# Three products of batch 1 split once more by Strassen's scheme, in a hand-scheduled cross-attention and LoRA feed-forward kernel

## The chip, the core and the metric

The kernel runs on one core of a Trainium2 chip. A core has five engines that work side by side: TensorE (PE in the profile) multiplies, with its weight loads in rows of their own (PEld); VectorE (DVE) and ScalarE (ACT) do arithmetic on tiles; GpSimd (POOL) does small things; SyncE (SP) issues every DMA of this kernel, in one queue, in order. Tiles lie in SBUF with 128 partitions; TensorE writes its sums to PSUM, of which the kernel has 8 banks of 128 x 512 fp32. The metric is the device time of one execution in microseconds (us). Each time given is the median of several runs, or, where it is said, the time of the one execution that the profiler recorded.

## The reference

Inputs are x (2 x 1024 x 2048), a context ctx (2 x 2048 x 2048), two scales and zero points, a weight W (2048 x 2048) with bias, a router (8 x 2048) and LoRA matrices A (8 experts x 16 x 2048) and B (8 x 2048 x 16). Cut to what matters:

```python
q = lambda v, s, z: (clip(round(v / s + z), 0, 255) - z) * s
x = x + q(layernorm(x), s1, z1) @ q(ctx, s2, z2)       # per batch: 1024x2048 @ 2048x2048
y = layernorm(x)
w = top-2 of softmax(y @ W_router.T), normalised, spread over the 8 experts
lora = einsum('ter,eor,te->to', einsum('td,erd->ter', y, A), B, w) * 2
x = x + y @ W.T + bias + lora                          # 1024x2048 @ 2048x2048
```

The second product is the expensive one. The kernel keeps y and W as two fp16 halves each (a high part and the rest), so that every product of y and W is three fp16 products: low*high, high*low and high*high.

## The kernel before

The two batches follow each other. In each, the first product (`gemm1` in batch 0, `gemm1w` in batch 1) is added to x, the rows are normalised, `y_prep` makes the left operands of the second product, and `g2` multiplies them with W.

The second product uses one level of Strassen's scheme (in Winograd's form). A block is a pair p of 128-row tiles (4 pairs), 2048 inner rows cut in halves of 8 x 128, and 1024 output columns cut in halves of 512. The outputs are done in two passes f = 0 and f = 1 of 1024 columns each (`cp`); batch 0 takes cp 0 and then 1, batch 1 cp 1 and then 0. In place of 8 products of blocks there are 7, with the left operands a11, a12, a22, s1, s2, s3, s4 (tiles `y_<name>`, made by `y_prep`: normalise, add, split in two fp16 halves (`nat`), turn by a DMA transpose) and right operands of sums of W's blocks, made by `w_step` for every inner step k. The seven stand in four groups (`GROUPS`); a group runs over 8 steps k, within it over the 4 pairs p, and each (k, p, product) is three matmuls of 512 columns (line 1407). At the end of a group `EVAC` has VectorE add PSUM banks to the output tiles (line 1435, `xr`), and `LORA` adds the LoRA product (line 1423). In pass 0 the last group is X += a22 @ (the fourth sum of W); in pass 1 a22 stands in the third group beside s3, and a12 alone in the fourth.

`w_step` loads rows of W in fp32, forms the sums on VectorE, scales and rounds the high half (`hi`, line 444, ACT or DVE) and makes the low half (`lo`, line 1211, DVE). Of pass 1 of batch 0 it writes fp16 halves to DRAM (`store_w`, tiles `made`), and pass 0 of batch 1, which needs the same sums, loads those (`w <- made`).

x itself is written to DRAM (`spill`) when y is made and comes back as `xr` (`reload`) for the last additions; `put` writes the finished rows out.

What sets the order: nothing is written down by hand. Every operation is a task with an engine, a guessed duration, the buffers it reads and writes and a due time `prio`. `Plan.order` (line 184) plays the program through with these guesses, keeps a heap of events, and at each moment gives each free engine the most urgent task that is ready and finds its buffers. The tasks are then issued in the order of their planned starts; on the chip every engine keeps its order and waits only for what it needs. The guesses are the constants at the head of the file: `RATE` the DMA rate, `LAND`, `STORE_LAND`, `TURN_LAND` the time from the last byte to the semaphore, `TURN_COST` and `TURN_ISSUE` the transposes. All big tiles share 49 buffers of 4 KB per partition (`SLOTS["u"]`); three narrow tiles (`byte`) are handed out in turn.

## Time and profile before

| | us |
|---|---|
| median of 3 runs (lowest, highest) | 912.36 (911.86, 913.17) |
| the profiled execution | 910.92 |
| its span, first to last instruction | 909.1 |
| PE busy in it | 896.0 (99%) |
| DVE busy | 708.0 (78%) |
| ACT busy | 388.7 (43%) |
| DMA queue 1, share of 16 engines' span | 86.8% |
| granted TensorE clock, mean | 1.00 |

A line of the groups reads: line of the kernel, engine, operation, tile written, tiles read, shapes, how many | busy time in us, mean ns of one | idle time before them and what ended it. Matmuls are pipelined: one of 512 columns lasts 379 ns in the records but the next one starts after 216. What a matmul costs is therefore read from a run of them in the timeline: the time of the run less one duration, over the number less one. In the table of windows a row gives a stretch, its length, and for each engine its busy time and number of instructions, then the granted clock, the DMA engines' mean share and GB/s.

### The profile page before, as it was taken

How to read it: one execution, taken by the hardware profiler on the slowest of the kernel's cores; microseconds unless marked ns; L12 is line 12 of the kernel's file. 1: busy time of each engine (PE TensorE's matmuls, PEld its weight loads, DVE VectorE, ACT ScalarE, POOL GpSimd, SP SyncE). 2: the span in 40 equal slices, each digit the busy share in tenths (PEclk: the TensorE clock that was granted, in tenths of full speed). 3: DMA queues.
4: the chain of work that ended last, by engine and by line, in shares of the span. 5: the costliest groups of instructions: out<-in, count | busy, mean ns of one | idle time of the engine just before them, and what ended most of it. 6: DMA issues, size and time to landing. Idle time of an engine off the chain costs nothing.

```text
span 909.1 us, 12499 instructions
## 1 busy us (share of the span) xinstructions
PE 896.0 (99%) x4542; PEld 432.4 (48%) x4542; DVE 708.0 (78%) x1305; ACT 388.7 (43%) x445; POOL 47.4 (5%) x199
## 2 busy tenths in 40 slices
PE   8899999999999999999999999999999999999998
PEld 6344446474444444444444444556444444444443
DVE  8989999999499966999889979999543363899131
ACT  4875976525144221323686776754100021324000
POOL 1014000000000000002540000000000000000000
PEclk9999999999999999999999999999999999999999
DMA  9999999998999999999999748999994169883021
GB/s 327 387 386 278 348 285 225 245 265 226 255 362 325 314 395 406 380 369 345 301 343 323 243 170 235 228 169 222 308 283 109 50 224 371 288 337 134 6 93 46
DMA packets 223917, 241.02 MB, mean 265 GB/s; under 512 B 146032, under 2 KB 158320, under 8 KB 223856
## 3 DMA queue, kind: packets, MB, share of 16 engines
q1 hardware_dynamic: 223856, 240.23, 86.8%
q8 instruction: 35, 0.57, 0.3%
q14 instruction: 26, 0.21, 0.1%
HBM read 163.65 MB, written 41.94 MB: 226 GB/s over the span
## 4 chain that ended last, share of the span: by engine, by line
PE 85%; DVE 9%; DMA 3%; issue 1%; SPq 1%; ACT 0%; DVEq 0%; ACTq 0%
PE X L1406 34%; PE Y L1406 27%; PE g L829 11%; PE gX L949 3%; PE ph L1067 3%; PE gY L949 2%; DVE x L858 2%; PE X L1423 2%; PE Y L1423 2%; PE ph L1071 1%; DMA x<-in_x_dram 1%; DVE byte L455 1%; DMA bs<-in_cx_dram 1%; DVE sm L478 1%; DVE bt L920 1%
## 5 line engine op out<-in xcount | busy, mean ns | idle before, releaser
L1406 PEld LDWEIGHTS <-y_s 128*128 128x128 f16 x1536 | 150.3, 98 | 181.0
L1406 PE MATMUL Y<-w,y_s 128*128 128x512 f16 x768 | 206.6, 379 | 0.0
L1406 PE MATMUL X<-w,y_s 128*128 128x512 f16 x768 | 206.3, 379 | 0.0
L1406 PE MATMUL X<-w,y_a 128*128 128x512 f16 x768 | 189.1, 379 | 0.2 <-DVE w L1211 0.2
L1406 PEld LDWEIGHTS <-y_a 128*128 128x128 f16 x1152 | 112.1, 98 | 132.6 <-issue 0.5
L829 PE MATMUL g<-b,at 128*128 128x512 f16 x512 | 112.5, 379 | 4.7 <-DVE b L469 3.6
L1406 PE MATMUL Y<-w,y_a 128*128 128x512 f16 x384 | 103.2, 379 | 0.0
L444 ACT ACTIVATE w<-wb,gW 128x1024 f16<-128x1024 f32 (+1 forms) x46 | 50.0, 1091 | 111.1 <-DVE wb L1282 32.9
L1435 DVE SCALAR_TENSOR_TENSOR xr<-X,uW,xr 128x512 f32<-128x512 f32 x64 | 46.8, 746 | 46.9 <-PE X L1423 25.7
L829 PEld LDWEIGHTS <-at 128*128 128x128 f16 x512 | 49.7, 98 | 64.3 <-issue 4.2
L1435 DVE SCALAR_TENSOR_TENSOR xr<-Y,uW,xr 128x512 f32<-128x512 f32 x42 | 31.1, 745 | 53.8 <-PE Y L1423 53.8
L1211 DVE SCALAR_TENSOR_TENSOR w<-wb,gW,w 128x1024 f16<-128x1024 f32 (+1 forms) x48 | 57.0, 1194 | 6.0 <-ACT w L444 5.9
L444 ACT ACTIVATE byte<-bs,sc,rec 128x1024 uint8<-128x1024 f32 x40 | 48.3, 1236 | 13.5 <-DMA bs<-in_cx_dram 8.6
L444 ACT ACTIVATE w<-wt,gW 128x1024 f16<-128x1024 f32 x15 | 17.0, 1145 | 78.5 <-DVE wt L1258 38.7
L478 DVE BATCH_NORM_STATS2 sm<-x 128x6 f32<-128x512 f32 x64 | 40.9, 683 | 5.5 <-ACT q L444 4.2
L877 ACT ACTIVATE byte<-x,sm 128x1024 uint8<-128x1024 f32 x32 | 36.4, 1139 | 10.4 <-DVE x L858 6.8
L444 ACT ACTIVATE nat_s<-yt_a 128x1024 f16<-128x1024 f32 x31 | 31.9, 1049 | 20.0 <-DVE yt_a L1026 14.7
L949 PEld LDWEIGHTS <-at 128*128 128x128 f16 x256 | 25.0, 98 | 29.8
L1026 DVE TENSOR_TENSOR yt_a<-yt_a,yt_a 128x1024 f32<-128x1024 f32 x32 | 38.7, 1221 | 0.0
L1018 DVE TENSOR_TENSOR nat_s<-yt_a,nat_s 128x1024 f16<-128x1024 f32 x32 | 38.2, 1224 | 0.0
L1067 PE MATMUL ph<-ar,y_a 128*128 128x272 f16 x192 | 35.7, 279 | 0.0
L1071 PE MATMUL ph<-ar,y_a 128*128 128x136 f16 x192 | 34.6, 223 | 0.0
(196 smaller groups left out, 1107.1 us busy)
## 6 DMA issues: line engine op xcount, KB each, us to landing
bs<-in_cx_dram SPq DMA_DIRECT2D x64, 512.0 KB, 10.5
wt<-in_wT_dram SPq DMA_DIRECT2D x64, 512.0 KB, 7.4
wn<-in_wT_dram SPq DMA_DIRECT2D x32, 512.0 KB, 9.1
x<-in_x_dram SPq DMA_DIRECT2D x30, 512.0 KB, 8.4
spill<-x SPq DMA_DIRECT2D x28, 512.0 KB, 4.4
xr<-spill SPq DMA_DIRECT2D x28, 512.0 KB, 8.5
wb<-in_wT_dram SPq DMA_DIRECT2D x24, 512.0 KB, 7.8
out_dram<-xr SPq DMA_DIRECT2D x24, 512.0 KB, 4.0
```

Source lines behind the costliest of these rows:

```text
L444: nc.scalar.activation(o, i, AF.Copy if c is None else AF.Identity, scale=1.0 if a is None else a, bias=0.0 if c is None else c,)
L478: nc.vector.bn_stats(st[:, 2 * h + c], b.ap()[:, c * C : (c + 1) * C])
L829: nc.tensor.matmul(ps.ap(), aT.ap()[:, k, :], S["b", c, k // 4].ap()[:, k % 4, :], start=k == 0, stop=k == KT - 1,)
L877: nc.scalar.activation(low(sq), xb.ap(), AF.Square, bias=a[:, 22 + j : 23 + j], accum_out=a[:, 24 + 2 * j + h : 25 + 2 * j + h],)
L949: nc.tensor.matmul(ps.ap(), a()[:, 4 * h + k, :], w.ap()[:, k, :], start=fresh and h + k == 0, stop=h == 1 and k == 3, skip_group_check=True,)
L1018: lambda: nc.vector.tensor_tensor(n.ap()[:, 1], t.ap(), n.ap()[:, 0], ALU.subtract),
L1026: add("DVE", 1.22, lambda: nc.vector.tensor_tensor(dst.ap(), a.ap(), c.ap(), op), r=[a, c], w=[dst])
L1067: nc.tensor.matmul(ph.ap()[:, : 2 * AR], y[half].ap()[:, 0, k, :], ar[:, kr, :], start=kk == 0, stop=False,)
L1071: nc.tensor.matmul(ph.ap()[:, AR : 2 * AR], y[half].ap()[:, 1, k, :], ar[:, kr, :AR], start=False, stop=kk == KT - 1,)
L1211: lambda: nc.vector.scalar_tensor_tensor(w.ap()[:, 1, lo:up], src(), g, w.ap()[:, 0, lo:up], ALU.mult, ALU.subtract),
L1406: nc.tensor.matmul(ps.ap(), y.ap()[:, a, k, :], w.ap()[:, q, j * C : (j + 1) * C], start=k == 0 and fresh and i == 0, stop=k == HK - 1 and ...
L1435: nc.vector.scalar_tensor_tensor(xs, ps.ap(), uW[:, cp : cp + 1], xs, ALU.mult, ALU.add)
```

## The change

1. Three of the fourteen block products of batch 1 (pass 0: a22; pass 1: a22 and a12) are no longer done by `g2` in its last group but by a new function `quarters`, which splits each once more: pairs of row pairs (2q, 2q+1), inner halves of 4 x 128, column halves of 256. Seven products of quarters take the place of eight; each is 12 matmuls of 256 columns (4 inner steps, three fp16 products) into a bank `X2`, `Y2` or into `X`. `LEVEL2` says which; `TABLE`, with a third entry in `GROUPS`, `LORA` and `EVAC`, leaves a22 and a12 out of pass 1's groups.
2. Their left operands are made by `y_quarters` from x, read back from `spill`: two extra turned tiles per pair of pairs and product (`q31`, `q24`). The four tiles a12 are written to DRAM in pass 0 (`y_out`) and read again in pass 1 (`y_in`).
3. Their right operands come from DRAM: a12's from W, a22's from two sums of W in fp32, which batch 0 stores (`store_t4`, tiles `t4`). Batch 0's pass 0 also reads its own third group's partial sum back (`wb <- t4`) instead of forming it again from rows of W. Pass 1's third group in batch 1 loads two 512-column pieces (`ws`) and makes one sum.
4. The scheduler: other constants; a store that is read later counts as done 2 us later; a transpose occupies the DMA from another moment; a `byte` tile goes back when its last user is issued, not in turn.

The diff, cut:

```diff
@@ -71,7 +71,16 @@
 PACE = .9
 TURNS = 4
 FAST = 4
-TMM = 0.12
+TMM = 0.08
+MM2 = 0.1095
+LEVEL2 = {(0, 0): (), (0, 1): (), (1, 0): ("a22",), (1, 1): ("a22", "a12")}
+TABLE = {(0, 0): 0, (0, 1): 1, (1, 0): 0, (1, 1): 2}
+YOUT = ((), ("a12",))
+T4 = (True, True)
+YO_T = 10.0
+YFAR = 60.0
+YQ = ((), ("a22", "a12"))
+SLOW_Q = 1.2
 SP_D = 10.0
 HC = 4.0
 PUT = 10.0
@@ -88,17 +97,20 @@
 SP_T = 5.0
 HOP = 0.7
 DMA_SLACK = 3.0
-RATE = 374e3
+RATE = 390e3
 SLOW_W = 1.18
 SLOW_C = 1.03
-LAND = 2.1
-STORE_LAND = 1.15
-TURN_LAND = 0.65
-TURN_COST = 1.0
-TURN_ISSUE = 1.5
+LAND = 1.5
+STORE_LAND = 1.35
+STORE_WAIT = 2.0
+TURN_LAND = 0.97
+TURN_COST = 1.35
+TURN_WHOLE = 1.95
+TURN_HEAD = {1: 0.9, 2: 1.6}
+TURN_ISSUE = 1.4
 RING = 5
 MERGE = 2.5
-WHOLE_ISSUE = 1.8
+WHOLE_ISSUE = 2.0
 TURN_RING = 2
 NEXT = {"DVE": 0.08, "ACT": 0.1}
 
@@ -290,7 +302,9 @@
                                 if room < 0 or len(group) > 1:
                                     end = max(end, at)
                                     break
-                        dma_free = max(end + 0.2, dma_free) + t.dma * len(group)
+                        begin = now + (TURN_HEAD[len(group)] if t.turn else t.dur + 0.2)
+                        dma_free = max(begin, dma_free) + (
+                            TURN_WHOLE if len(group) > 1 else t.dma)
                         done = dma_free + (
                             TURN_LAND if t.turn else STORE_LAND if t.store else LAND
                         )
@@ -321,7 +335,7 @@
                                     wake(b.last)
                         for x in t.succs:
                             x.left -= 1
-                            x.ready = max(x.ready, t.done)
+                            x.ready = max(x.ready, t.done + (STORE_WAIT if x.store and x.succs else 0.0))
                             if not x.left:
                                 for e in x.durs:
                                     bisect.insort(ready[e], (x.prio, x.seq, x))
@@ -357,9 +371,7 @@
 
     def byte(name):
         def make():
-            ring = rings["byte"]
-            ring.append(ring.pop(0))
-            return ring[-1]
+            return rings["byte"].pop(0)
 
         return Buf("byte", make, 1, name)
@@ -993,6 +1005,61 @@
...
+    def y_quarters(S, b, q, o):
+        yt = []
+        j = int(o[1]) - 1
+        for p in (2 * q, 2 * q + 1):
+            s = S["s2", p]
+            d = S["spill", 2 * p + j, 1]
+            t = buf("u", [P, HD], F32, f"yq_{o}_{b}_{p}")
+            load(t, t.ap, d.ap, HD * 4, [t], r=[d])
+            affine(t.ap, t.ap, HD, [(s, [j])], [t], scale=lambda s=s: s.ap()[:, 10 + j : 11 + j],
+                   bias=lambda s=s: s.ap()[:, 12 + j : 13 + j])
+            yt.append(t)
+        a, c = yt
+        lo = lambda t: t.ap()[:, :C]
+        up = lambda t: t.ap()[:, C:]
+
+        def comb(dst, x, y, op, r, w):
+            add("DVE", 0.69, lambda: nc.vector.tensor_tensor(dst(), x(), y(), op), r=r, w=[w])
+
+        comb(lambda: up(c), lambda: lo(c), lambda: up(c), ALU.add, [], c)
+        comb(lambda: lo(c), lambda: lo(a), lambda: lo(c), ALU.subtract, [a], c)
+        comb(lambda: lo(a), lambda: up(c), lambda: lo(a), ALU.subtract, [c], a)
+        comb(lambda: up(a), lambda: up(a), lambda: lo(a), ALU.subtract, [], a)
+        y_emit(S, b, 2 * q, o + "q31", c)
+        y_emit(S, b, 2 * q, o + "q24", a)
+
@@ -1043,7 +1095,7 @@
         emit("s4", t5)
         for i in (2 * p, 2 * p + 1):
             for h in range(2):
-                if h == b and p >= SPILL0:
+                if h == b and p >= SPILL0 and f"a{1 + i % 2}2" not in YQ[b]:
@@ -1170,11 +1222,20 @@
             hh.ap().rearrange("p t h c -> p (t h c)")))
 
     made = {}
+    whole_t4 = {}
     STORED = {
         0: ((1, 1, 1),),
         1: ((0, 0, 1), (1, 1, 2)),
-        2: ((0, 0, 3), (1, 0, 2)),
+        2: ((0, 0, 3), (1, 0, 2)) if "a22" not in LEVEL2[1, 0] else ((1, 0, 2),),
...
+    def store_t4(k, cp, s, cap):
+        if cp not in whole_t4:
+            whole_t4[cp] = Buf(
+                "dram", lambda: dram.tile([P, HK, C], F32, name=f"t4_{cp}"), HK)
+        d = whole_t4[cp]
+        load(d, lambda: d.ap()[:, k], lambda: s.ap()[:, :C], C * 4, [(d, [k])], r=[s],
+             store=True, cap=cap)
 
@@ -1229,11 +1289,25 @@
                 add("DVE", 0.69,
                     lambda: nc.vector.tensor_tensor(
                         s.ap()[:, :C], s.ap()[:, :C], s.ap()[:, C:], ALU.subtract), w=[s])
+                if not b and T4[f]:
+                    store_t4(k, cp, s, t + PUT_W)
...
                 add("DVE", 0.69,
                     lambda: nc.vector.tensor_tensor(
                         s.ap()[:, :C], s.ap()[:, C:], s.ap()[:, :C], ALU.subtract), w=[s])
+            elif not b and T4[f]:
+                s = buf("u", [P, HD], F32, f"wb_{n}")
+                d = whole_t4[cp]
+                load(s, lambda: s.ap()[:, :C],
+                     wT[(HK + k) * P : (HK + k + 1) * P, cp * HD : cp * HD + C],
+                     C * 4, [s])
+                load(s, lambda: s.ap()[:, C:], lambda: d.ap()[:, k], C * 4, [s], r=[(d, [k])], far=WFAR)
+                add("DVE", 0.69,
+                    lambda: nc.vector.tensor_tensor(
+                        s.ap()[:, :C], s.ap()[:, :C], s.ap()[:, C:], ALU.subtract), w=[s])
+                if "a22" in LEVEL2[1, 1]:
+                    store_t4(k, cp, s, t + PUT_W)
@@ -1251,6 +1325,16 @@
...
+        if grp == 2 and "a22" in LEVEL2[b, f]:
+            s = buf("u", [P, 2, C], F32, f"ws_{n}")
+            load(s, s.ap, wT.rearrange("(h k p) n -> k p h n", h=2, p=P)[k][
+                :, :, cp * HD + C : (cp + 1) * HD], HD * 4, [s], slow=SLOW_W, far=WFAR)
+            add("DVE", 0.69,
+                lambda: nc.vector.tensor_tensor(
+                    s.ap()[:, 0], s.ap()[:, 1], s.ap()[:, 0], ALU.subtract), w=[s])
+            hi(lambda: s.ap()[:, 0], 0, C, [s])
+            lo(lambda: s.ap()[:, 0], 0, C, [s])
             return
@@ -1283,8 +1367,156 @@
...
+            if not b and "a22" in LEVEL2[1, 0]:
+                store_t4(k, cp, bot, t + PUT_W)
...
+    QUARTERS = (
+        ("b11", "", 0, 0), ("t1", "q31", 4, 0), ("t2", "q24", 0, 0), ("b22", "q24", 4, 0),
+        ("t3", "q31", 0, 0), ("b21", "", 4, 0), ("t4", "", 4, 1),
+    )
+
+    def quarters(S, b, f, cp, t, o):
+        g = gW[:, cp : cp + 1]
+        H2 = C // 2
+        raw, made_w = {}, {}
+        for h, n in ((0, 0), (0, 1), (1, 1), (1, 0)):
...
+            load(s, s.ap, src, HD * 4, [s], r=r, slow=SLOW_Q, far=WFAR)
+            raw[h, n] = s
...
+        def split(name, s):
+            w = buf("u", [P, 2, HD], F16, f"wq{o}_{cp}_{name}")
+            affine(lambda: w.ap()[:, 0], flat(s), HD, [s, (scale_b, [cp])], [w], scale=g)
+            add("DVE", 1.28,
+                lambda: nc.vector.scalar_tensor_tensor(
+                    w.ap()[:, 1], flat(s)(), g, w.ap()[:, 0], ALU.mult, ALU.subtract),
+                r=[s, (scale_b, [cp])], w=[w])
+            made_w[name] = w
+
+        def comb(d, x, y):
+            add("DVE", 1.22,
+                lambda: nc.vector.tensor_tensor(
+                    flat(d)(), flat(x)(), flat(y)(), ALU.subtract), r=[x, y], w=[d])
+
...
+        t3 = buf("u", [P, 4, H2], F32, f"wq{o}_{cp}_d3")
+        split("b11", b11)
+        comb(t3, b22, b12)
+        comb(b12, b12, b11)
+        split("t1", b12)
+        t2 = b11
+        comb(t2, b22, b12)
+        split("t2", t2)
+        split("b22", b22)
+        split("t3", t3)
+        split("b21", b21)
+        comb(b21, b21, t2)
+        split("t4", b21)
...
+                y = S["y", 2 * q + side, o + op]
+                if name in ("b11", "t2", "t3"):
+                    if name == "b11":
+                        inner["X", q] = bank(f"X2_{b}_{cp}_{q}{o}")
+                    ps, col, fresh = inner["X", q], 0, name == "b11"
+                elif name == "t1":
+                    inner["Y", q] = bank(f"Y2_{b}_{cp}_{q}{o}")
+                    ps, col, fresh = inner["Y", q], 0, True
+                else:
+                    ps = S["X", 2 * q + side]
+                    col, fresh = (H2 if name == "b22" else 0), False
+
+                def mm(ps=ps, col=col, fresh=fresh, y=y, w=w, k0=k0):
+                    for k in range(4):
+                        for i, (a, h) in enumerate(((1, 0), (0, 1), (0, 0))):
+                            nc.tensor.matmul(
+                                ps.ap()[:, col : col + H2], y.ap()[:, a, k0 + k, :],
+                                w.ap()[:, h, k * H2 : (k + 1) * H2],
+                                start=fresh and k + i == 0, stop=k == 3 and i == 2,
+                                skip_group_check=True,
+                            )
+
+                add("PE", 12 * MM2, mm, r=[y, w], w=[ps], prio=t)
+                t += 12 * MM2
+                xP, xQ = top[2 * q], top[2 * q + 1]
+                if name == "b11":
+                    ev(ps, 0, H2, xP, 0)
+                elif name == "t1":
+                    ev(ps, 0, H2, xP, H2)
+                    ev(ps, 0, H2, xQ, H2)
+                elif name == "t2":
+                    ev(ps, 0, H2, xP, H2)
+                elif name == "t3":
+                    ev(ps, 0, H2, xQ, 0)
+                    ev(ps, 0, H2, xQ, H2)
+                elif name == "b21":
+                    ev(ps, 0, C, xP, 0)
+                    put(S, b, f, cp, 4 * q + side0, t)
+                elif name == "t4":
+                    ev(ps, 0, C, xQ, 0)
+                    put(S, b, f, cp, 4 * q + 2 + side0, t)
+        return t
 
@@ -1364,6 +1596,11 @@
             (("Y", "a22", True), ("X", "s3", False)),
             (("X", "a12", True),),
         ),
+        (
+            (("X", "a11", True), ("Y", "s1", True)),
+            (("X", "s2", False), ("Y", "s4", False)),
+            (("X", "s3", False),),
+        ),
     )
     LORA = (
```

The lines left out hold `y_emit` (moved out of `y_prep`, unchanged), `y_out` and `y_in` (one store and one load of a turned tile), the narrow additions `ev` (the operation of line 1435 with 256 or 512 columns), the LoRA products at the head of `quarters` (as many as before, moved there from the last group), the third entries of `GROUPS`, `LORA` and `EVAC`, and the calls in the main loop.

## The prediction

> **What bounds the kernel now.** I read the page's busy table and slices first, then the waits of TensorE, the windows, the timeline for what one matmul costs, and the groups for durations.
>
> ```profile
> PE 896.0 (99%) x4542; PEld 432.4 (48%) x4542; DVE 708.0 (78%) x1305; ACT 388.7 (43%) x445; POOL 47.4 (5%) x199
> PE   8899999999999999999999999999999999999998
> DVE  8989999999499966999889979999543363899131
> DMA  9999999998999999999999748999994169883021
> ```
>
> TensorE works in every slice; VectorE and the DMA engines have holes in batch 1's second product, the right third. The waits say the same; they add up to 9 us, and two of them (gX, gY) lie near 485 us, the only ones behind the lead-in above half a us:
>
> ```profile
> PE g L829 <- DVE b L469: 3.6, 3, 2.3
> PE turn L794 <- DVE qn L469: 1.7, 3, 1.3
> PE gX L949 <- DVE as L903: 1.2, 1, 1.2
> PE warm L771 <- POOL ones L393: 1.0, 1, 1.0
> PE g L829 <- ACT at L444: 0.9, 2, 0.7
> PE gY L949 <- DVE x L858: 0.3, 1, 0.3
> ```
>
> So only fewer or shorter matmuls, or a shorter lead-in, can shorten the time; everything else matters where it makes TensorE wait. The windows show where there is room:
>
> ```profile
> 320.00:400.00 80.00, 80.00 (x372) 36.32 (x371) 60.50 (x71) 21.46 (x20) 0.00 (x0) 1.00 1.04 394
> 640.00:760.00 120.00, 120.00 (x557) 54.41 (x556) 52.79 (x95) 13.36 (x14) 0.00 (x0) 1.00 0.70 200
> 780.00:800.00 20.00, 20.00 (x95) 9.05 (x93) 19.62 (x27) 7.08 (x7) 0.00 (x0) 1.00 0.79 278
> 840.00:905.00 65.00, 65.00 (x303) 29.36 (x300) 14.59 (x22) 0.00 (x0) 0.00 (x0) 1.00 0.10 42
> ```
>
> (The columns are PE, PEld, DVE, ACT, POOL where it has work, clock, DMA share, GB/s; the row at 780 is one of the fullest of VectorE.) VectorE is idle for 67 of 120 us from 640 and for 50 of 65 from 840; the DMA engines are full at 320 to 400, where the weights of batch 0's second pass are loaded and stored.
>
> **What a matmul costs.**
>
> ```profile
> 16.84 1.47 PE L780 MATMUL warm<-ones 128*128 128x256 f16 x12
> 185.00 0.28 PE L1067 MATMUL ph<-ar,y_a 128*128 128x272 f16 x1
> 185.11 0.22 PE L1071 MATMUL ph<-ar,y_a 128*128 128x136 f16 x1
> 895.78 5.56 PE L1406 MATMUL X<-w,y_a 128*128 128x512 f16 x25
> ```
>
> 512 columns: (5.56 - 0.379) / 24 = 0.216 us from start to start. 256 columns, a weight load before each: (1.47 - 0.273) / 11 = 0.109. Those loads fetch the same weights every time; with new weights each, 272 columns take 0.116 (0.11 between the starts shown), and 136 columns 0.06, so loads of 98 ns hide even there. I take 0.109; the bad end is 0.116.
>
> **The products.** Each of the three removed products is 4 pairs x 8 k x 3 = 96 matmuls of 512 columns; its replacement 7 x 2 x 12 = 168 of 256. The LoRA matmuls move with them and keep their number. Removed 288 x 0.216 = 62.2, added 504 x 0.109 = 54.9: 7.3 us off TensorE's line (at 0.116: 3.7). With TensorE busy 80 of 80 and 65 of 65 us there, all of it lies on the path.
>
> **VectorE and ScalarE.** A product needs 7 low halves at 1.283 (the 1024-column row of L1211), 4 sums at 1.22, 12 narrow and 4 wide additions out of PSUM. Wide ones are 0.746 (L1435). No row shows a narrow one; the same kind of operation on 32 columns takes 0.248 (L575), so a line through both gives 0.48; the ends are 0.37 (half of 0.746) and 0.746. Sum: 9.0 + 4.9 + 5.8 + 3.0 = 22.7, three times 68. The quarter tiles: 16 sums of 512 columns at 0.69, 8 low halves at 1.22, 20.8. Gone in batch 1: 20 wide additions, 8 halves at 0.754, and 8 x 1.75 where pass 1's third group makes one sum and 512 columns in place of two and 1024: 34.9. Net +54 in batch 1; batch 0 saves 8 x 1.22 (L1241) = 10. ScalarE gains 24 (21 high halves at 1.146) + 18 (8 normalisations at 1.233, 8 high halves at 1.05) less 9 us, with most of its time free. +54 fits into 67 + 50 us of holes. In the changed kernel's order I summed these durations per 20 us of matmul time: the fullest stretches hold 20 to 22 us (700 to 740, 760 to 800, 820 to 860), as do those of before (780 to 820: 21.7 and 21.9), which the trace shows as 19.6 and 19.0 busy, because successive operations overlap, with no wait of TensorE. So 0 us, and if this cover failed, the price under the second rival. [...]
>
> **Banks.** Bank X2 is drained after b11, t2 and t3 and refilled in between. From the end of one pair's step to its bank's next use lie three steps of 12 x 0.109, 3.9 us. VectorE needs 0.5 for the drain, and at worst ends a 1.28 and a 0.75 operation first: 2.5. Hidden.
>
> **DMA.** Batch 1 gains 7.3 MB (8 x spill loads, 8 tiles out and in, 2 more spills, 12 quarters of W; less the `made` and `ws` pieces) and 16 transposes; its holes (share 0.70 over 120 us, 0.10 over 65) hold 94 us of them. Every store that is read again lies at least 38 us of matmul time before its load in the changed order, so SP, where all loads queue behind a waiting one, does not stop there (47 more issues at 0.3 to 0.5 us each, on a queue that is mostly idle); the landing takes 6.4 us (`made`), 4.4 (`spill`). In the full stretch 320 to 400 the order holds 30.4 MB against 29.9: 1.3 us of transfer at 394 GB/s, hidden by loads that run ahead. The plan now counts on 390 GB/s. [...]
>
> **The new order of everything.** The constants reshuffle batch 0 too. Where the plan expects TensorE to stand, several VectorE operations are issued between two neighbouring matmuls. Before: 3.3 us of them at 68 us of matmul time (all places counted so), 2.8 at 390, 3.4 at 474; the trace shows waits of 0.2, 0 and 1.6 there, 1.8 of 9.5. After: 3.3 at 68, 2.2 at 347, 6.2 at 390 to 393, none at 474: 11.7. At 347 X's additions stand behind two weight sums, and the next group waits for their banks. Where the wait at 474 goes (first sums of batch 1's operands), the banks' additions of the next groups come next; their distances in the order are as before. By the same ratio 2.2, so +0.4; ends -1.8 (no wait) and +9.9 (all of it). Lead-in: the second b tile comes 2.1 us of VectorE work sooner, less 0.7 for a copy taken from ScalarE, which takes over a 1.24 us rounding; the first 40 us of matmul time hold 80.5 us of both engines against 81.4. I take 0, ends -1.4 and +1.2. The tail: last addition, last 256 KB store (2.1 us), as before; the other column halves leave 55 us sooner. 0.
>
> **Sum.** 910.9 (the profiled execution, span 909.1 and 1.8 around it) - 7.3 + 0.4 = 904.0. The median stands 1.4 above that execution: 905.4.
>
> **Rivals.**
> - *The bursts are real* (0.14). The plan's own waits at 347 and 390 to 393 come true in part: 3 to 7 us, because VectorE is in order and X's additions stand behind 1.28 us halves. For: 2.2 and 6.2 us of work between two matmuls. Against: 390 held 2.8 before and cost nothing. Time 908 to 912, say 909.5.
> - *VectorE paces the three products* (slower, 0.12). If the weight quarters aren't ready ahead, a product lasts its 22.7 us of VectorE instead of 18.3: +4.4 each, 912.4 - 7.3 + 13.2 = 918. It decides from 3.0 us per product (7.3 + 1.8 over three). For: between 820 and 860 the second product shares VectorE with the third's halves. Against: the last half of the first product is issued 1.4 us of matmul time before it starts but 17 before its use, the second's and third's 16 and 9 before the start, and 22.7 us of work shrinks by 0.09 per operation in a dense run (0.66 between the starts of 0.74 us additions at 400).
> - *Narrow matmuls don't pay* (0.04): at 62.2 / 504 = 0.123 us each the gain is nothing, 912.4. The 272-column row at 0.116 is the argument against.
> - *A better lead-in* (0.04): 1.4 and 1.8 more, 902 or less.
>
> **How the numbers follow.** The forecast (0.66) spans 902 to 908. A measurement here tells 0.2% (1.8 us) from nothing: faster is under 910.5. Faster: 0.66 + 0.04 + 0.10 of the bursts = 0.80; same: 0.04 + 0.04 = 0.08; slower 0.12. The range 902 to 912 holds forecast and bursts, 0.80, and the bad end of the matmul row (909).
>
> **What would show it.** TensorE's instructions 216 more, busy time about 889; 256-column matmuls 0.109 apart in runs; VectorE's busy time near 750 with tenths of 5 to 9 where 3 to 5 stood in the right third; no wait of X2 or Y2 above 1 us. Wrong: waits of TensorE on L1683 (the wide additions' new line) near 360 and 400 us that sum to over 3 us, on the narrow additions in the products, or a loaded tile late.

## The result, and the profile after

| | before | after |
|---|---|---|
| median, us (lowest, highest; 4 runs each) | 912.11 (910.22, 913.17) | 934.62 (933.13, 936.24) |
| the profiled execution, us | 910.92 | 935.37 |
| its span, us | 909.1 | 933.6 |
| granted TensorE clock, mean | 1.000 | 0.993 |

The change makes the kernel slower: the ratio of the times is 1.0249, with a 95% interval of 1.0224 to 1.0275. The forecast was 905.4 us, in a range of 902 to 912.

The page of the changed kernel, with the busy table, four rows of the slices and the shares of the chain that ended last:

```profile
PE 896.7 (96%) x4758; PEld 453.9 (49%) x4758; DVE 751.0 (80%) x1371; ACT 420.3 (45%) x473; POOL 49.8 (5%) x199
PE   8899999999998799999999999989999989999998
DVE  8988999989486664989689988899817788697983
PEclk9999999999999799999999999999999999999999
DMA  9999999999999899999899757999999669882862
PE 65%; DVE 14%; DMA 12%; ACT 3%; issue 3%; SPq 1%; POOL 1%; DVEq 0%; ACTq 0%; POOLq 0%
```

TensorE has the 216 matmuls more that were counted, and VectorE is busy for 43 us more (44 were summed). TensorE's busy time is 896.7 us and not the 889 that was expected, in part because the spells of slow matmuls, shown below, count as busy. But TensorE now has slices of 7 and 8 tenths at 300 us, 610 us and 750 us, the clock row has a 7 in it, and the chain that ended last runs through TensorE for 65% of the span, where it was 85% before. The longest waits of TensorE behind the lead-in (engine, what it wanted to do and the line, the operation that released it: us in total, how often, the longest):

```profile
PE X L1654 <- DVE xr L1683: 4.2, 2, 2.5
PE X L1654 <- DVE x L1683: 3.3, 1, 3.3
PE X L1450 <- DVE xr L1683: 3.1, 2, 2.9
PE X L1654 <- DMA y_a<-nat_a: 2.7, 1, 2.7
PE ph L1123 <- DMA y_a<-nat_a: 2.1, 1, 2.1
PE arn L557 <- DVE a L553: 1.9, 1, 1.9
PE Y L1654 <- DVE xr L1683: 1.8, 4, 0.6
```

They are waits for additions of PSUM banks (L1683), for turned tiles a (`y_a`) and for the router's operand, and most lie far from the new products: of the twelve, only the two on L1450, at 751 and 752 us, stand at the head of one.

**Where the 24.5 us of span come from.** The same reckoning is used for every run below. Between neighbouring matmuls in the timeline, the distance from start to start beyond the cadence of that width (0.216 us for 512 columns, 0.116 for 272, 0.109 for 256, 0.059 for 136) is a gap, so a spell of slow matmuls counts too; the gaps are summed by place. Before, all gaps together are 13.0 us, 10.6 of them in the lead-in. After, they are 44.6. So 31.6 us more gaps less 7.3 us fewer matmuls make +24.3, and the span grew by 24.5. The matmuls gave what they were to give, and four times as much was lost in waits and in the slow matmuls behind them.

The largest place is 300 to 316 us, the passage from pass 0 to pass 1 of batch 0, 440 us ahead of the first new product. VectorE's timeline there (start, duration, what; in brackets the idle time ahead and what ended it):

```profile
301.81 0.69 DVE L1307 TENSOR_TENSOR wb<-wb 128x512 f32<-128x512 f32 x1 [2.14 <-DMA wb<-t]
302.42 0.74 DVE L1683 SCALAR_TENSOR_TENSOR xr<-X,uW,xr 128x512 f32<-128x512 f32 x1
...
309.05 0.69 DVE L1307 TENSOR_TENSOR wb<-wb 128x512 f32<-128x512 f32 x1 [2.64 <-DMA wb<-t]
309.66 0.16 DVE L673 TENSOR_REDUCE wacc<-wacc 128x1 f32<-128x16 f32 x1
309.74 0.74 DVE L1683 SCALAR_TENSOR_TENSOR x<-X,uW,x 128x512 f32<-128x512 f32 x1
```

VectorE keeps its order here: it stands 2.14 and 2.64 us on the sum of a weight block (L1307) whose t4 part is still on its way from DRAM, and the additions that would free the banks stand behind that sum. TensorE's gaps are 2.6, 1.9 and 3.7 us. The t4 loads that the two rows with brackets wait for were issued at 292.56 and 302.79 us and landed 9.2 and 6.2 us later. SP's longest waits in the same stretch (280 to 312 us):

```profile
SPq L437 <- DMA t<-wb: 5.6, 2, 5.0
SPq L437 <- DMA wn<-in_wT_dram: 2.7, 1, 2.7
```

The wait of 2.7 us on a load of W, and one of 1.2 us on ScalarE behind it, stand ahead of the load at 302.79. Both waits on stores of t4 come later: the one of 5.0 us begins at 306.09, when the loads that TensorE ends up waiting for are already out. So in the changed kernel it is the late loads of t4, and not SP's waits on its stores, that can be tied to these three gaps.

Then the clock falls. The windows (columns as before: PE, PEld, DVE, ACT, POOL, clock, DMA share, GB/s), and with them the two stretches in which VectorE had its holes:

```profile
640.00:760.00 120.00, 116.74 (x619) 57.90 (x618) 81.80 (x126) 32.25 (x37) 0.00 (x0) 0.99 0.90 224
840.00:905.00 65.00, 65.00 (x370) 36.00 (x368) 57.25 (x70) 23.89 (x22) 0.00 (x0) 1.00 0.58 162
306.00:311.00 5.00, 1.71 (x5) 0.50 (x4) 2.36 (x5) 2.48 (x4) 0.00 (x0) 0.50 0.74 266
311.00:316.00 5.00, 5.00 (x14) 1.78 (x13) 2.75 (x5) 0.00 (x0) 0.00 (x0) 0.51 0.76 233
```

From 311 to 316 us TensorE is never idle, and still only 14 matmuls start in 5 us, at a clock of 0.51. VectorE's holes did take the new work: 82 us busy in the 120 from 640 where 53 were, 57 in the 65 from 840 where 15 were, and in the second of them TensorE does not stand at all.

### The profile page after: what moved, and what is told of

Read it like the earlier page. It is cut to its first block, busy times and chain, and to the rows that moved or that the text cites. A ratio compares the mean times of both kernels' runs of the same rounds, so it can differ in the third digit from the quotient of the medians.

```text
span 933.6 us, 13157 instructions
## 1 busy us (share of the span) xinstructions
PE 896.7 (96%) x4758; PEld 453.9 (49%) x4758; DVE 751.0 (80%) x1371; ACT 420.3 (45%) x473; POOL 49.8 (5%) x199
## 4 chain that ended last, share of the span: by engine, by line
PE 65%; DVE 14%; DMA 12%; ACT 3%; issue 3%; SPq 1%; POOL 1%; DVEq 0%; ACTq 0%; POOLq 0%
PE X L1654 23%; PE Y L1654 18%; PE g L841 9%; PE gX L961 3%; PE gY L961 2%; PE ph L1119 2%; DMA wn<-in_wT_dram 2%; DMA wc<-in_wT_dram 2%; DMA wb<-in_wT_dram 2%; DMA wb<-t 2%; DMA wt<-in_wT_dram 1%; PE X L1493 1%; DVE w L1271 1%; DMA q<-q 1%; DMA bs<-in_cx_dram 1%
## 5 line engine op out<-in xcount | busy, mean ns | idle before, releaser
L1654 PE MATMUL X<-w,y_s 128*128 128x512 f16 x768 | 202.1, 379 | 1.4 <-DVE w L1271 1.4
L1654 PE MATMUL X<-w,y_a 128*128 128x512 f16 x576 | 150.1, 386 | 10.2 <-DVE xr L1683 4.2
L1654 PEld LDWEIGHTS <-y_a 128*128 128x128 f16 x864 | 84.4, 99 | 113.9 <-issue 14.7
L456 ACT ACTIVATE w<-wb,gW 128x1024 f16<-128x1024 f32 (+1 forms) x38 | 40.6, 1079 | 104.0 <-DVE wb L1356 50.7
L1654 PE MATMUL Y<-w,y_a 128*128 128x512 f16 x288 | 77.4, 379 | 1.8 <-DVE xr L1683 1.8
L1683 DVE SCALAR_TENSOR_TENSOR xr<-X,uW,xr 128x512 f32<-128x512 f32 x53 | 38.7, 744 | 28.8 <-PE X L1654 28.8
L456 ACT ACTIVATE byte<-bs,sc,rec 128x1024 uint8<-128x1024 f32 x42 | 50.5, 1235 | 17.8 <-DMA bs<-in_cx_dram 16.6
L1271 DVE SCALAR_TENSOR_TENSOR w<-wb,gW,w 128x1024 f16<-128x1024 f32 (+1 forms) x40 | 46.6, 1173 | 8.2 <-ACT w L456 8.0
L889 ACT ACTIVATE byte<-x,sm 128x1024 uint8<-128x1024 f32 x32 | 36.4, 1139 | 10.9 <-DVE x L870 8.4
L664 ACT ACTIVATE wn<-wn 128x1024 f32<-128x1024 f32 x21 | 22.1, 1050 | 39.2 <-DMA wn<-in_wT_dram 39.2
L456 ACT ACTIVATE nat_s<-yt_a 128x1024 f16<-128x1024 f32 x30 | 30.8, 1049 | 18.4 <-DVE yt_a L1078 14.2
L1557 DVE TENSOR_TENSOR xr<-xr,bb 128x1024 f32<-128x1024 f32 x28 | 33.4, 1218 | 2.1 <-DMA bb<-in_bias_dram 2.1
```

The costliest lines, as they stand in the source:

```text
L456: nc.scalar.activation(o, i, AF.Copy if c is None else AF.Identity, scale=1.0 if a is None else a, bias=0.0 if c is None else c,)
L889: nc.scalar.activation(low(sq), xb.ap(), AF.Square, bias=a[:, 22 + j : 23 + j], accum_out=a[:, 24 + 2 * j + h : 25 + 2 * j + h],)
L1271: lambda: nc.vector.scalar_tensor_tensor(w.ap()[:, 1, lo:up], src(), g, w.ap()[:, 0, lo:up], ALU.mult, ALU.subtract),
L1654: nc.tensor.matmul(ps.ap(), y.ap()[:, a, k, :], w.ap()[:, q, j * C : (j + 1) * C], start=k == 0 and fresh and i == 0, stop=k == HK - 1 and ...
L1683: nc.vector.scalar_tensor_tensor(xs, ps.ap(), uW[:, cp : cp + 1], xs, ALU.mult, ALU.add)
```

## The experiments

Two theories at the start. A: the new plan (part 4: constants and rules of the scheduler) makes TensorE wait. B: the products' operands do (quarter tiles, t4 sums, a12 out and in). A third came up on the way, O: the order before happened to be a rare one without stalls, and almost any other order of the same work has some. Ratios are against the kernel before, run on the same chip. "Old constants" means that all of part 4 but the handing out of the `byte` tiles is put back.

All runs in one table: median, ratio with its interval, then TensorE's gaps in us by place in the profiled run. The gaps are those of one execution; executions of one kernel lie 1 to 5 us apart in most rows, 9 in plan_only and before_rate378 and 14 in prod_dma_old. A difference of a few us between two cells is therefore no result by itself.

| kernel | us | ratio (95%) | lead-in, to 50 | 50-270 | 270-345 | 345-480 | 480-570 | 570-660 | from 660 | all |
|---|---|---|---|---|---|---|---|---|---|---|
| before | 912.11 | 1 | 10.6 | 0.7 | 0.0 | -0.1 | 2.1 | -0.1 | -0.2 | 13.0 |
| after | 934.62 | 1.0249 (1.0224-1.0275) | 9.6 | 9.2 | 12.1 | 2.4 | 2.4 | 3.5 | 5.5 | 44.6 |
| plan_only | 926.31 | 1.0195 (1.0148-1.0241) | 9.9 | 4.5 | 5.4 | 0.3 | 4.4 | 0.6 | 0.1 | 25.3 |
| products_only | 916.58 | 1.0065 (1.0047-1.0083) | 11.1 | 0.7 | 5.1 | 0.0 | 2.7 | 3.5 | 2.0 | 25.1 |
| prod_turn_old | 930.70 | 1.0214 (1.0197-1.0231) | 9.6 | 5.0 | 9.8 | 1.7 | 4.1 | 5.9 | 4.1 | 40.1 |
| prod_dma_old | 925.56 | 1.0115 (1.0069-1.0160) | 9.8 | 3.9 | 8.0 | 2.8 | 3.0 | 5.7 | 1.7 | 34.8 |
| prod_no_readback | 923.96 | 1.0133 (1.0115-1.0151) | 10.4 | 0.8 | 10.1 | -0.1 | 3.7 | 6.9 | 1.6 | 33.4 |
| prod_yout_late | 919.10 | 1.0082 (1.0065-1.0098) | 11.4 | 1.1 | 5.0 | -0.1 | 2.2 | 6.4 | 1.8 | 27.8 |
| only_a22_first | 919.62 | 1.0086 (1.0069-1.0103) | 10.4 | 1.3 | 0.2 | -0.1 | 2.1 | -0.1 | 9.8 | 23.8 |
| only_a12 | 915.16 | 1.0038 (1.0019-1.0056) | 10.9 | 0.7 | 0.6 | -0.1 | 1.9 | 5.7 | -0.2 | 19.6 |
| before_land20 | 912.06 | 1.0016 (1.0006-1.0026) | 10.9 | 1.1 | 0.0 | 0.2 | 1.5 | -0.1 | -0.2 | 13.3 |
| before_rate378 | 915.95 | 1.0059 (1.0040-1.0078) | 10.9 | 0.9 | 5.5 | -0.1 | 1.6 | -0.1 | -0.2 | 18.5 |
| prod_land22 | 921.04 | 1.0107 (1.0090-1.0124) | 10.9 | 2.5 | 3.1 | 1.8 | 5.9 | 4.9 | 3.0 | 32.0 |
| prod_slow_plan | 919.82 | 1.0095 (1.0079-1.0112) | 11.6 | 1.7 | 1.6 | -0.1 | 4.8 | 10.4 | 1.0 | 30.8 |
| no_left | 913.41 | 1.0029 (1.0017-1.0042) | 10.3 | 0.7 | 6.4 | -0.1 | 2.6 | 4.4 | -0.1 | 24.3 |
| no_t4 | 914.85 | 1.0047 (1.0030-1.0063) | 10.3 | 0.7 | 1.1 | -0.1 | 4.4 | 3.1 | 3.5 | 22.9 |
| no_left_t4 | 911.32 | 0.9989 (0.9974-1.0005) | 10.2 | 0.8 | 2.0 | -0.1 | 3.9 | 3.0 | -0.1 | 19.8 |
| only_a12_land20 | 913.47 | 1.0020 (1.0006-1.0035) | 10.9 | 1.5 | 0.0 | -0.1 | 1.1 | 4.1 | -0.1 | 17.3 |
| prod_pin_hold | 915.19 | 1.0045 (1.0028-1.0061) | 11.5 | 0.7 | 2.9 | 0.1 | 3.8 | 2.0 | 4.2 | 25.2 |
| only_a12_pin | 909.77 | 0.9977 (0.9966-0.9988) | 11.5 | 0.7 | 0.5 | -0.1 | 2.2 | -0.1 | -0.1 | 14.6 |

In each row the sum of the matmuls (-7.3 us with three products, -2.4 with one) and the gaps beyond 13.0 gives the span to within 0.7 us: for products_only -7.3 + 12.1 = +4.8, and its span is 914.0 against 909.1.

### The plan alone, the products alone

```diff
-LEVEL2 = {... (1, 0): ("a22",), (1, 1): ("a22", "a12")}     # plan_only: level 2 off
+LEVEL2 = {... (1, 0): (), (1, 1): ()}                       # (TABLE, YOUT, YQ, T4 to match)
```

> The changed kernel with the three products put back as they were (no second level, no tiles of y or sums of W written out and read back): what is left of the change is part 4, the scheduler's constants, its rule for transposes and the byte tiles. Theory A (the new plan itself makes TensorE wait): the changed kernel's TensorE stood 31.5 us longer between matmuls than the one before (44.8 against 13.3), so this one is far slower than before, 925 to 943 us. Theory B (the waits come with the added products, their DMA traffic and the t4 sums read back in batch 0): 908 to 915. If both contribute, something between.

```diff
-TMM = 0.08     -RATE = 390e3   -LAND = 1.5   -STORE_LAND = 1.35   -STORE_WAIT = 2.0
+TMM = 0.12     +RATE = 374e3   +LAND = 2.1   +STORE_LAND = 1.15   +STORE_WAIT = 0.0
-TURN_LAND = 0.97  -TURN_COST = 1.35  -TURN_ISSUE = 1.4  -WHOLE_ISSUE = 2.0
+TURN_LAND = 0.65  +TURN_COST = 1.0   +TURN_ISSUE = 1.5  +WHOLE_ISSUE = 1.8
-begin = now + (TURN_HEAD[len(group)] if t.turn else t.dur + 0.2)
+begin = end + 0.2
```

(products_only; `dma_free` is advanced as before, too.)

> The changed kernel with the scheduler's old constants and its old rule for transposes and stores; the products, their tiles and the traffic stay. Theory A (the new plan makes TensorE wait): the prediction's own sum, 902 to 909 us. Theory B (the products' traffic and the read-back do): 925 to 937.

Measured: 926.3 and 916.6. The plan alone costs 15 us, the products under the old plan 5.5, and the changed kernel's 22.5 is near their sum. plan_only falls in the range of theory A, products_only in neither range: both parts contribute, and the plan the more. The plan alone does the work of the kernel before and has 25.3 us of gaps against 13.0, the larger ones at 79, 149, 295 to 299 and 495 to 508 us. The products' 5.5 us are their 7.3 us of gain less 12.1 us of new gaps, most of them at 283 to 326, at 603 and at 737 to 743 us.

### Which constants

The two halves of the last diff, each put back by itself with the products in place: the lines of the transposes (`TURN_*`, `WHOLE_ISSUE`, `begin`) in prod_turn_old, `RATE`, `LAND`, `STORE_LAND` and `STORE_WAIT` in prod_dma_old.

> The changed kernel with only the transposes' constants and rule put back (129 transposes issued in place of 138, since more of them are joined in pairs); the new DMA rate and landing times stay. Theory A1 (under the new rule fewer transposes are joined, SP and the DMA queue fall behind before 300 and 750 us): 902 to 915. Theory A2 (390 GB/s and 1.5 us of landing leave loads too little time): 925 to 937.

> The changed kernel with only the DMA rate, the landing times and the 2 us after a store put back; the transposes' new rule stays, and so do the 138 transposes. Theory A1 (transposes): 925 to 937. Theory A2 (rate and landing): 902 to 915.

Measured: 930.7 with the transposes' constants put back, 925.6 with those of rate and landing (and 916.6 with both). Neither A1 nor A2 holds: each promised that its own group alone would bring the time to 915 or less. Two more parts were not separated: `TMM` kept its new value in both runs, and the new handing out of the `byte` tiles stands in every kernel made from the changed one. Rate and landing weigh more (from 44.6 to 34.8 us of gaps when they go, against 40.1 for the transposes), but the nudges further down move the time by up to 5 us for no reason that a constant has, so the shares are not to be trusted to a few microseconds.

### One part of the products at a time

prod_no_readback (old constants) forms batch 0's fourth sum from rows of W again and only stores it:

```diff
-T4 = (True, True)
+T4 = (False, False)
@@ w_step, pass 0, last group, formed from two rows @@
+                if not b and "a22" in LEVEL2[1, 1]:
+                    store_t4(k, cp, s, t + PUT_W)
```

> The kernel with the products and the old constants (916.6 us), but batch 0's pass 0 forms its fourth sum from rows of W again, as before the change, and stores only the result: 8 stores and 8 loads of t4 fewer, 8 more full rows of W loaded. With the old constants TensorE's gaps between 280 and 340 us are 4.9 us, none of them there before the change. Theory R (the chain t4 store, load, sum, behind which the additions of the banks stand on VectorE): those gaps fall under 1 us, 911 to 913. Theory T (the additional traffic of batch 0 as a whole, which goes up here by 2 MB): 916 to 919.

prod_yout_late (old constants) has `YO_T = 60.0` in place of 10.0.

> The kernel with the products and the old constants (916.6 us), but the four tiles a12 are written out 50 us later. In its trace TensorE waits 2.6 us at 603 us for a turned tile a whose transpose stands on SP behind those stores and two more spills. Theory Q (SP's queue: what stands ahead of the last transposes): the wait at 603 falls under 1 us, 913.5 to 915. Theory N (the transposes are late of themselves, by batch 1's fuller VectorE or DMA): unchanged, 916 to 918.

only_a22_first and only_a12 (old constants) keep one product each:

```diff
-LEVEL2 = {... (1, 0): ("a22",), (1, 1): ("a22", "a12")}
+LEVEL2 = {... (1, 0): ("a22",), (1, 1): ()}                 # only_a22_first; T4 (False, False)
+LEVEL2 = {... (1, 0): (), (1, 1): ("a12",)}                 # only_a12; T4 (False, False)
```

> Old constants, and only the first of the three products (pass 0 of batch 1, a22): its turned quarters, the t4 sums that batch 0's pass 1 stores, no read-back, no a12 tiles out and in. The matmuls give 96 x 0.216 - 168 x 0.109 = 2.4 us. If the products themselves are as costed and only what goes with the others makes the waits: 908.5 to 911. If each product brings a third of the 12 us of new waits: 912 to 914.

> Old constants, and only the third product (pass 1 of batch 1, a12): its right quarters come straight from W, nothing of batch 0 changes but the order; its a12 tiles go out and in and two more spills are made. The matmuls give 2.4 us. If the waits at 283 to 330 us come from t4 alone they are gone, and what stays is the wait at 603: 910 to 913. If a12's traffic does no harm: 908.5 to 910.

Measured: 924.0, 919.1, 919.6 and 915.2; every expectation missed, the hopeful and the cautious ones. Taking the read-back away made the place that it was to heal worse (10.1 us of gaps at 270 to 345, from 5.1), so theory R found no support; but this kernel also loads 8 more rows of W and has another order, and the run doesn't clear the read-back. One product has no gap in batch 0 and none at 600, but stands on its own operands, in the middle of the product (waits of TensorE in only_a22_first):

```profile
PE Y_1a L1493 <- DMA y_a22q<-nat_a22q: 3.4, 1, 3.4
...
PE X L1493 <- DVE wqa_t L1404: 1.8, 1, 1.8
```

The other one has its gaps at 597 and 641 us. And prod_yout_late turned out not to be the experiment that it was meant to be: in its trace the four stores `yout` still stand among the transposes, at 563, 595 (two of them) and 610 us. The plan gives SP any store that is ready when SP is idle in the plan, up to 120 us ahead of its due time (`HORIZON`), so a later due time did not take them away. The question is taken up again below.

### The same work in another order

before_land20 is the kernel before with `LAND = 2.0` for 2.1, before_rate378 with `RATE = 378e3` for 374e3; prod_land22 is products_only with `LAND = 2.2`, prod_slow_plan with `RATE = 360e3`, `LAND = 2.6`.

> The kernel before with one guess of its plan nudged, the landing time from 2.1 to 2.0 us; the same work, and an order in which some 350 operations stand 0.3 us or more elsewhere and 4 of them 2 us or more. Theory O (the order before happens to have no stall, and nearly any other order of the same work, which the plan thinks as good, has some waits of 1 to 4 us and a spell of half clock behind them): 914 to 922. Theory W (the new waits come from the work that the change adds and from constants far from the truth): 910.5 to 913.

> The kernel before with the DMA rate of its plan nudged from 374 to 378 GB/s; the same work in a slightly other order. Theory O: 914 to 922. Theory W: 910.5 to 913.

> The products with the old constants (916.6 us), and the landing time nudged from 2.1 to 2.2 us. Theory O: the waits change their places and their sum by several us either way, 910 to 922. Theory W: they stay at 283 to 330, at 603 and at 740, and the time within 1.5 us of 916.6.

> The products with a plan that reckons with slower DMA than the old constants (360 GB/s and 2.6 us of landing against 374 and 2.1), so that it orders loads earlier. If the waits come from too little margin of loads and transposes: fewer of them, 906 to 912. Theory O (any order has its stalls): 912 to 920.

Measured: 912.1, 916.0, 921.0, 919.8. So theory O is true in half: the kernel before loses 1 us by one nudge and 5 by the other, with no work added. What the second one opened is at the same passage as in the changed kernel (TensorE's waits of before_rate378 from 270 to 345 us):

```profile
PE wsum L665 <- DVE wacc L661: 1.8, 1, 1.8
PE X L1406 <- DVE x L1435: 1.5, 1, 1.5
PE X L1406 <- DVE w L1211: 1.3, 3, 0.6
```

The three products under four plans (916.6, 919.1, 919.8, 921.0) lie 4.5 us apart, and the best of them is 5.5 us behind the kernel before. A plan that reckons with slower DMA, and so orders loads earlier, does not help either; it trades the gaps at 270 to 345 (1.6) for those at 570 to 660 (10.4).

### Operands left out

no_left multiplies the plain tiles in place of the quarter tiles and makes none; no_t4 stores no sums and loads blocks of W in their place; no_left_t4 does both (old constants in all three). only_a12_land20 is only_a12 with `LAND = 2.0`.

```diff
-YQ = ((), ("a22", "a12"))                                   # no_left
+YQ = ((), ())
-                y = S["y", 2 * q + side, o + op]
+                y = S["y", 2 * q + side, o]
-T4 = (True, True)                                           # no_t4
+T4 = (False, False)
-            if o == "a12":                                  # source of the right quarters
+            if True:
-            if not b and "a22" in LEVEL2[1, 0]:
-                store_t4(k, cp, bot, t + PUT_W)
```

> The products under the old constants (916.6 us) without making their left quarter tiles: the products multiply the plain tiles a22 and a12 in their place, so that 8 loads, 16 sums, 16 roundings, 16 halves and 16 transposes and two spills of batch 1 are left out (the products' values are then not the reference's). The matmuls are the same number. Theory L (the left operands' transposes push SP's queue and make the waits at 603 and 740, 3.5 + 2.1 us): 910 to 912. Theory D (the t4 traffic of batch 0 makes most): 915 to 917. Theory O (the order as such): 912 to 920 with waits at new places.

> The products under the old constants without the t4 sums: nothing is stored or read back in batch 0, and batch 1 loads blocks of W in place of the sums (the values of a22's products are then not the reference's). Batch 0 then does what it did before the change. Theory D: the 4.9 us of waits at 283 to 330 go, 911 to 913. Theory L: 915 to 917. Theory O: 912 to 920 with waits at new places.

> Both left out: the products as matmuls, additions and right halves alone. If the gain of the matmuls is real and on the path and the waits come from the operands: 912.1 - 7.3 = 904 to 907. Theory O (the order as such costs it): 908 to 918.

> The third product alone (915.2 us) with the landing time of the plan at 2.0 in place of 2.1 us, the nudge that moved the kernel before by 1 us. Theory O: another draw of the order, 909 to 917, its waits elsewhere than at 597 and 641. Otherwise within 1.5 us of 915.2, the same two waits.

Measured: 913.4, 914.9, 911.3 and 913.5. All four lie in the ranges of theory O, which are wide; theory L and theory D miss theirs by 0.1 to 2 us. Without t4 the gaps at 270 to 345 fall from 5.1 to 1.1; without the left tiles they are 6.4 with t4 and 2.0 without it. So t4 goes with about 4 us there in both pairs, each kernel with its own order. Without the left tiles the gaps from 660 on fall from 2.0 to -0.1. Even with both left out the kernel is only level with the one before (0.9974 to 1.0005), not at the 904 to 907 us of the hopeful expectation, with 2.7 us at 600 for a turned tile that comes late. What no_left, no_t4 and no_left_t4 still share there are the four stores of a12. only_a12_land20 loses its gap at 641 and keeps one of 2.7 us at 597: another order, and the same place.

How a store can stop the engines shows in products_only. SP's timeline from 287 us:

```profile
287.49 1.30 SPq L437 DMA_DIRECT2D t<-wb  x2
288.84 0.53 SPq L437 DMA_DIRECT2D wb<-t  x1
295.54 0.38 SPq L437 DMA_DIRECT2D wn<-in_wT_dram  x1
```

SP issues nothing for 6.1 us, and the view of its waits names the store: `t<-wb`, 6.1 us, once. The load that stands, `wn`, reads nothing of t4. The buffer that it is to fill still holds a sum that the store at 287.49 is reading, and that store lands 7.98 us after its issue, at 295.47. The plan had counted the store as done 1.15 us after its transfer, so the buffer was given away. VectorE meets the same thing (its timeline in the same kernel):

```profile
296.21 0.49 DVE L463 TENSOR_SCALAR w<-wb,gW 128x512 f16<-128x512 f32 x1 [2.12 <-DMA t<-wb]
296.73 0.75 DVE L1271 SCALAR_TENSOR_TENSOR w<-wb,gW,w 128x512 f16<-128x512 f32 x1
297.40 0.75 DVE L1683 SCALAR_TENSOR_TENSOR x<-X,uW,x 128x512 f32<-128x512 f32 x1
```

The second store, issued at 288.28, lands 7.83 us later at 296.11; only then may VectorE write `w` into that buffer, and the bank's addition at 297.40 stands behind it. That is TensorE's gap of 2.8 us at 295; ahead of it VectorE had also stood 2.2 us at 290 on a load of t4 (`wb<-t`).

### The stores held back

```diff
-    load(d, d.ap, y.ap, HD * 4, [d], r=[y], store=True, cap=when)             # YO_T = 60.0
+    load(d, d.ap, y.ap, HD * 4, [d], r=[y], store=True, cap=when, far=2.0)
-    b.last = max(getattr(b, "last", 0.0), t.done)                             # prod_pin_hold alone
+    b.last = max(getattr(b, "last", 0.0), t.done + (3.0 if t.store else 0.0))
```

With `far` the store may not be issued more than 2 us ahead of its due time.

> The products under the old constants (916.6 us), with two edits of the plan: a buffer that a store reads counts as free 3 us later than the store's guessed landing, and the four a12 stores may not be issued before their due time, so that they stand behind the transposes (at 620 to 631 us of matmul time, where before they stood at 543 to 574). If the two causes are right: the 5.1 us of gaps at 270 to 345 fall to 2 or less, the 3.5 us at 570 to 660 under 1, 908 to 912. Theory O (the order as such): waits of the same sum at new places, 913 to 921.

> The third product alone under the old constants (915.2 us), its four a12 stores held back behind the transposes in the same way. If the stores among the transposes make the waits at 597 and 641 (5.7 us with the half clock behind the second): under 1 us there, 909 to 911. Theory O: 912 to 917.

Measured: 915.2 and **909.8**. The third product alone, with its stores out of the transposes' way, beats the kernel before by 0.12 to 0.34%, and the changed kernel by some 25 us. TensorE's waits from 560 to 700 us in only_a12, of which only_a12_pin has none, and SP from 572 us in only_a12:

```profile
PE X L1654 <- DVE x L1683: 2.0, 1, 2.0
PE X L1654 <- DMA y_a<-nat_a: 1.7, 1, 1.7
```

```profile
572.44 0.34 SPq L437 DMA_DIRECT2D yout_a<-y_a  x1
572.87 0.39 SPq L437 DMA_DIRECT2D wc<-in_wT_dram  x1
573.72 7.34 SPq L446 DMA_TRANSPOSE y_a<-nat_a  x2
581.11 0.57 SPq L437 DMA_DIRECT2D spill<-x  x1
581.77 3.20 SPq L446 DMA_TRANSPOSE y_a<-nat_a  x2
585.08 0.59 SPq L437 DMA_DIRECT2D yout_a<-y_a  x1
...
587.71 7.30 SPq L446 DMA_TRANSPOSE y_a<-nat_a  x2
595.11 3.01 SPq L1023 DMA_TRANSPOSE y_a<-nat_a  x1
598.22 0.52 SPq L437 DMA_DIRECT2D yout_a<-y_a  x1
```

and in only_a12_pin:

```profile
575.16 3.83 SPq L446 DMA_TRANSPOSE y_a<-nat_a  x1
579.08 0.54 SPq L437 DMA_DIRECT2D spill<-x  x1
579.67 3.98 SPq L446 DMA_TRANSPOSE y_a<-nat_a  x1
583.75 3.11 SPq L1023 DMA_TRANSPOSE y_a<-nat_a  x1
586.96 0.53 SPq L437 DMA_DIRECT2D xr<-spill  x1
588.46 7.12 SPq L446 DMA_TRANSPOSE y_a<-nat_a  x5
```

The joined transpose (L1023) goes out at 583.8 in place of 595.1, the stores from 636 to 643 us. It is this transpose that TensorE waits for in only_a12: it lands at 599.53, and the matmul starts at 599.58. The gaps at 570 to 660 fall from 5.7 to nothing.

The edit moved more than the stores, though. Between 572 us and the joined transpose only_a12 has two a12 stores, which take SP 0.9 us (and SP stands 0.8 us ahead of the first), and six other transposes. only_a12_pin has two other transposes there, and so has the kernel before, where the joined one goes out at 581.89. Most of the 11 us by which it is late go to the four more transposes ahead of it, with SP's waits for their tiles. So holding the stores back took the gap at 597 away; whether the stores themselves or the order that the plan made round them caused it was not separated. The gap at 641, a wait for a bank's addition, was already gone in only_a12_land20, with its stores where they were. And this is one kernel out of many orders of nearly the same work, where a nudge alone is worth 1 to 5 us, so theory O is not excluded here either.

In the three-product version the same edit, together with the longer hold, goes with 2.0 us at 570 to 660, from 3.5. The longer hold of stored buffers, by a guess of 3 us, brought the place at 270 to 345 from 5.1 to 2.9, though SP still stands 5.4 us on one t4 store there; the waits at 734 to 739 us, ahead of the first product, then cost 4.2. That version misses the hopeful expectation in all three numbers (915.2, 2.9 and 2.0 for 908 to 912, 2 or less and under 1), and its gaps sum to what they were, 25.2 us, as theory O has it.

## Why the prediction was wrong

Point by point, as the prediction has them:

- **What a matmul costs, the products: right.** The third product in the changed kernel runs without a wait: 168 starts from 911.09 to 929.32 us, 0.1092 apart. The first two of its runs of 12 (start, the time from the first start to the last end):

```profile
911.09 1.47 PE L1493 MATMUL X_0a<-wqa_b,yin_a 128*128 128x256 f16 x12
912.40 1.47 PE L1493 MATMUL X_1a<-wqa_b,yin_a 128*128 128x256 f16 x12
```

  The 7.3 us, and 2.4 for one product, are in every balance above.
- **VectorE and ScalarE: the sizes right, the cover wrong at one spot.** The net work was summed as +44 us and is +43. The narrow addition, interpolated as 0.48 us, is 0.480; the wide one 0.745 (lines of the groups):

```profile
L1432 DVE SCALAR_TENSOR_TENSOR xr<-X_0a,uW,xr 128x256 f32<-128x256 f32 x12 | 5.7, 480 | 8.4 <-PE X_0a L1493 8.4
L1432 DVE SCALAR_TENSOR_TENSOR xr<-X,uW,xr 128x512 f32<-128x512 f32 x7 | 5.1, 745 | 1.5 <-PE X L1493 1.5
```

  Inside the products the holes covered it. At the head of the first product they did not: the additions of the old banks stand behind 1.28 us halves of the new weights (L1404), of which the one at 749.33 had waited 3.5 us for ScalarE, and TensorE stands 3.1 us at 752. That is the rival *VectorE paces the three products* at one point, not over three products; its 918 us was not the mechanism that decided.
- **Banks: right** in the changed kernel (its longest wait on X2 is 0.3 us); in products_only the first filling of X2 waited 1.0.
- **DMA: wrong, in the sentence that SP "does not stop there".** I looked at the distance from a store to the load of the same data, 38 us and more, and that was long enough. I didn't look at the buffer that a store reads from until it lands: for t4 6.6 us after its issue in the median of the changed kernel's 24 stores, 6.0 in products_only, and there 7.98 for the one at 287.49 us. SP stood 5.0 us at one such buffer in the changed kernel, with no gap of TensorE that can be tied to it, and 6.1 in products_only, where VectorE stands 2.1 us on the next such buffer ahead of TensorE's gap of 2.8. Nor did I cost the 47 more issues where SP is not "mostly idle": between 560 and 606 us it carries the transposes on which TensorE waits next. In only_a12 one of them is late by 1.9 us of TensorE's time at 597, and with the a12 stores held back it is not; that the stores did it by themselves was not shown.
- **The new order of everything: wrong, and by most; this is the step that failed.** I took +0.4 us and bounded it by 9.9, from bursts of VectorE work between neighbouring matmuls. The plan alone measured +15, and the products under the old plan came with 12.1 us of new gaps, where the sum has 0.4 for the order and nothing for the traffic. Of the places that I had listed, 390 to 393 us of matmul time did come true: four waits of 0.3 to 0.65 us on bank additions at 422 to 429 us of the trace (1.8 us of waits, 2.4 of gaps, under the 3 to 7 of that rival); 347 did not. But that count sees only what VectorE has to do at a place if everything else is on time. It cannot see a load, a store's buffer or a transpose that is late, and the largest of the other waits followed such ones (300 to 316 and 611 us in the changed kernel, 295 and 603 in products_only). Of the signs of being wrong that I had named, the late tile came; the waits on L1683 came too, 1.8 us of them at the place named near 400 us (422 to 429 in this trace), but 10.6 at 303 to 310 and at 752. The bound of 9.9 us was no bound.
- **The lead-in and the tail: right.** The lead-in lost 1.0 us of gaps (I had taken 0, at best -1.4); from the last matmul's start to the span's end it is 4.3 us before and after.
- **320 to 400 us: right.** The stretch moves 362 GB/s with a share of 0.99 and TensorE has no gap of 0.1 us there.

What stays open: which of the new constants and rules does the harm in the plan alone, since two groups of them each do part of it, `TMM` and the `byte` tiles were not put back by themselves, and small nudges move the time by up to 5 us; how much of the products' 12.1 us of gaps belongs to their traffic and how much to the order as such; and why the passage at 270 to 345 us stalls under one order and not under another, beyond the t4 buffers that were seen.

## What to carry to other kernels

Where an engine is 99% busy, a change that reorders everything is not priced at its own operations: first ask what the order had been worth, by nudging the planner's constants with the same work (here 1 and 5 us), and take that as the least width of the range. For each store that is added, look at three things: what is issued behind it in the same queue, who waits for the buffer it reads, and how long it takes to land (here 6 to 8 us from its issue; the plan had counted 1.15 after the transfer). One product of the three, with its stores held behind the critical transposes, was 0.2% faster than the kernel before; all three, under every plan tried, were slower than it.

## What the runs showed of the hardware

In these runs a long wait of TensorE cost more than itself. Counted as gaps from start to start, all eight single waits of 3.0 us or more behind the lead-in (3.7 us at 307 and 3.1 at 752 in the changed kernel; by the view of waits 4.1 in prod_turn_old, 3.6 in prod_dma_old, 4.0 and 3.0 in prod_no_readback, 3.4 in only_a22_first, 3.5 in prod_slow_plan) were followed by a spell at half clock (0.51 from 311 to 316 us in the changed kernel, 0.54 from 738 to 741 in only_a22_first; the mean granted clock of the six executions is 0.993 to 0.996, of the kernel before 1.000), in which matmuls of 512 columns start 0.427 us apart and those of 256 columns 0.21: 4 to 13 matmuls, up to 2.7 us on top. Of the waits of 2.0 to 2.9 us that stood by themselves some 8 of 22 were (2.0 us at 752 in only_a22_first: some 15 slow matmuls of 256 columns, the clock 0.57 from 754 to 758; 2.2 at 641 in only_a12: 7; 2.9 at 611 in the changed kernel: none), and of the shorter ones that stood by themselves none (1.5 us at 518 in the changed kernel, for one). So 2.0 us was enough in one of these runs, and 2.9 us had no such spell behind it in another. Some kernels with such waits vary from run to run: prod_dma_old, with waits of 1.6 to 3.8 us, spreads from 916 to 930 us, the kernel before on the same chip from 910 to 913; that the half-clock spells make this spread was not shown.

The other row to keep is a price: a narrow addition out of PSUM measures 0.480 us and a wide one 0.745 (the groups of L1432 above). The line through the two, 0.215 us and 1.04 ns per column, is an estimate from these two widths alone.
